# A graph attention kernel: one-hot picks from keys kept in DRAM, and one copy with three predicated copies in place of a mask and additions

## The chip, the cores and the metric

The kernel runs on one core of one Trainium2 chip. The metric is the device time of one execution in microseconds, the median of several runs.

## The reference

Three layers of a graph transformer over 6250 nodes of 64 features and 206250 edges, sorted by destination. Per layer:

```python
q, k, v = x @ Wq + bq, x @ Wk + bk, x @ Wv + bv
e = edge_attr @ We
alpha = sum(q[dst] * (k[src] + e), -1) / sqrt(64)
w = softmax of alpha over the edges of each dst
x = segment_sum((v[src] + e) * w, dst) + x @ Ws + bs
x = relu(x)            # and a layer norm with gamma and beta after layers 0 and 1
```

At the end `layernorm(x0 + log_softmax(x))`.

## The kernel before

Edges are cut into 403 chunks of 512, a chunk into four tiles of 128 edges (`T = 4`), and four chunks make a batch (`LB = 4`): 100 whole batches and a rest. Nodes stand in 49 blocks of 128. `x` of a layer lies in DRAM, and, split into two parts whose sum is exact enough, in SBUF as `parts` (18 low blocks and 18 high blocks).

The features of the source nodes, `x[src]`, reach the tile `feat` of a batch in one of two ways. A *gather* is an indirect DMA that POOL issues, one for each tile of 128 edges (L578). A *pick* computes the same rows on PE: a one-hot of the source node against `parts`. In layer 0 the edges of each chunk are sorted (`sorter`, class `Move`, with `hit` one-hots and matmuls at L993 and L1002) so that tile 0 of a chunk has only sources in the low blocks and tile 3 only sources in the high ones; only those tiles can be picked. `PICKS` says how many of the sixteen tiles of a batch are picked: 3 in layer 0 and 6 in layers 1 and 2; so 13 and 10 tiles are gathered.

A pick works in groups of two tiles of the same kind (class `Picker`). `aim` multiplies `coef` with the batch's codes (`to`, loaded whole from `toS`, 128 rows) to put each edge's key, the place of its source node, on all 128 partitions in PSUM (L1182, two matmuls), and DVE compares it with `rank` for five groups of four blocks at once, which makes `hot` (L1196). `batch` multiplies `hot` with `parts`, ten matmuls a tile, eight of 256 columns and two of 128 (L1218). The result `ps_x` (layer 0: `ps_s`) has rows of four candidate blocks for each edge; DVE multiplies them with a mask `which` (L1229) and adds them up in two steps (L1232, L1233), the last of which writes `feat`. `aim` for the next group is called as a group's matmuls begin, so its one-hot is emitted one group ahead.

The order of instructions on each engine is written out by hand. A unit (one batch) goes: `sums` of the unit two before (L1522), `weights` of the unit before (L1510, L1512), `scores` (L1484, L1488, then L1498 on DVE and the exponential L1502 on ACT), then four `turn`s, which transpose the gathered features of one chunk each (L1473 on PE, L1476 on ACT). Between the turns stand the picks of the next batch. After each turn ACT copies the index of a later chunk into a `gate` (L609), and the gathers of that chunk wait for it; in layers 1 and 2 it is the chunk two batches later. As a batch's node groups end, `finish` computes the new `x` (L1334 and following). In layer 0 the sorter's steps (`move`) stand between the turns as well, one whole move a unit.

DMAs other than the gathers go out on SP's and ACT's queues in program order. `drain` writes the sorted codes of a batch to `toS` (L1017, ACT's queue), and `decode` loads them (L1608, SP's queue) up to three units ahead into one of four `to` tiles, which both `aim` and `scores` read.

## Time and profile before

| | |
|---|---|
| time, median of 3 runs | 4654.81 us (4653.18 to 4660.39) |
| profiled execution | 4656.6 us, span 4654.9 us |
| PE busy | 4216.7 us (91%) |
| DVE busy | 3829.2 us (82%) |
| POOL busy | 3337.9 us (72%) |
| ACT busy | 1995.7 us (43%) |
| mean granted TensorE clock | 0.966 |
| layer 0, 1 and 2 | about 0 to 1900, 1950 to 3250, 3300 to 4600 us |

Layer boundaries show in the forty slices of the page as the two dips:

```profile
PE   6889999999999999689999999999699999999996
POOL 6777777777777766277777777777477777777774
```

Each digit is the busy share of a slice of 116 us in tenths. A row of a group reads: line, engine, operation, output and input tiles, shape, count, then busy time in total, mean ns of one, and after the second bar the idle time of the engine just before them and what ended it. PE's ends are modelled and overlap, so the text works with the time from one start to the next. POOL's instruction is the issue of the gather, not its transfer.

### The profile page before, as it was taken

Reading aid. Unit: us, or ns where it says so; the run is one execution under the profiler, and the core shown is the slowest. Engines: PE = TensorE matmul, PEld = TensorE weight load, DVE = VectorE, ACT = ScalarE, POOL = GpSimd, SP = SyncE. Lnnn points to the kernel's source line nnn. Section 1 sums busy time; section 2 is a strip of 40 time slices with the busy share of each in tenths; the row PEclk is TensorE's granted clock in tenths of the full one; section 3 lists DMA queues with packets and bytes.
Section 4 is the critical chain, followed back from the end, with each engine's and each line's share of the span. In section 5 each row is a group of like instructions: output and inputs, shape, how many; then the busy total and the mean of one; then the engine's idle time right before and its main releaser. Section 6 shows DMA issues by size and latency. Waiting matters only on the chain.

```text
span 4654.9 us, 117245 instructions
## 1 busy us (share of the span) xinstructions
PE 4216.7 (91%) x41145; PEld 3111.6 (67%) x41145; DVE 3829.2 (82%) x9064; ACT 1995.7 (43%) x5733; POOL 3337.9 (72%) x3390
## 2 busy tenths in 40 slices
PE   6889999999999999689999999999699999999996
PEld 3445555555555555367888888887478778878874
DVE  6778888898888888478888888888478888888885
ACT  2455555555555555333333333333234333334443
POOL 6777777777777766277777777777477777777774
PEclk9999999999999999799999999999799999999997
DMA  8787777777777777445555565555356655656553
GB/s 188 192 210 184 188 204 188 189 195 200 199 198 193 192 197 189 125 102 132 137 139 137 138 144 138 140 138 129 86 128 143 141 135 135 138 130 143 136 135 81
DMA packets 769749, 725.47 MB, mean 156 GB/s; under 512 B 403478, under 2 KB 544880, under 8 KB 769156
## 3 DMA queue, kind: packets, MB, share of 16 engines
q1 hardware_dynamic: 572564, 480.73, 43.5%
q0 software_dynamic: 108160, 110.97, 12.7%
q10 hardware_dynamic: 88432, 126.17, 7.7%
q8 instruction: 334, 5.47, 0.5%
q14 instruction: 259, 2.12, 0.2%
HBM read 557.62 MB, written 159.87 MB: 154 GB/s over the span
## 4 chain that ended last, share of the span: by engine, by line


## 5 line engine op out<-in xcount | busy, mean ns | idle before, releaser
L578 POOL DMA_INDIRECT feat<-x,gate x2004 | 1924.4, 960 | 613.9 <-issue 471.5
L578 POOL DMA_INDIRECT feat<-in_x,gate x1328 | 1365.8, 1028 | 526.2 <-issue 317.1
L1218 PE MATMUL ps_x<-parts,hot 128*128 128x256 f32 (+1 forms) x11880 | 1567.1, 288 | 0.0
L1218 PEld LDWEIGHTS ps_x<-parts,hot 128*128 128x128 f32 x11880 | 1457.1, 193 | 0.0
L1476 ACT COPY featT<-ps_a 64x256 f32<-64x256 f32 x2380 | 872.4, 367 | 1305.8 <-PE ps_a L1473 1265.2
L1196 DVE TENSOR_TENSOR hot<-ps_m,rank 128x1280 fp32r<-128x1280 f32 x594 | 879.9, 1481 | 33.1 <-PE ps_m L1182 32.9
L993 PE MATMUL ps_x<-hit,thirds 128*64 128x512 bf16 x4800 | 637.7, 393 | 5.5 <-DVE hit L983 5.1
L1473 PE MATMUL ps_a<-ident,feat 128*128 128x128 f32 x2380 | 488.0, 283 | 64.0 <-DMA feat<-x,gate 40.4
L983 DVE TENSOR_SCALAR hit<-ruler,pos 128x512 bf16<-128x512 f16 x1600 | 504.6, 363 | 1.7 <-PE ps_m L1002 1.5
L1473 PEld LDWEIGHTS ps_a<-ident,feat 128*128 128x128 f32 x2380 | 281.9, 140 | 333.4 <-issue 287.5
L1229 DVE TENSOR_TENSOR rows_of_b<-ps_x,which 128x512 f32<-128x512 f32 x594 | 406.4, 684 | 88.1 <-PE ps_x L1218 87.1
L1502 ACT ACTIVATE prob<-ps_s,part 128x512 f32<-128x512 f32 (+1 forms) x306 | 210.6, 688 | 625.6 <-DVE part L1500 500.0
L1218 PE MATMUL ps_s<-parts,hot 128*128 128x256 f32 (+1 forms) x2680 | 392.3, 294 | 30.9 <-ACT prob L1502 30.9
L993 PEld LDWEIGHTS <-thirds 128*64 128x64 bf16 x4800 | 233.2, 111 | 230.5 <-issue 83.6
L1218 PEld LDWEIGHTS ps_s<-parts,hot 128*128 128x128 f32 x2680 | 340.8, 195 | 60.7 <-ACT prob L1502 40.7
L1498 DVE TENSOR_REDUCE most<-ps_s 128x1 f32<-128x512 f32 (+1 forms) x306 | 211.2, 690 | 189.4 <-PE ps_s L1488 181.4
L1232 DVE TENSOR_TENSOR rows_of_b<-rows_of_b 128x256 f32<-128x256 f32 (+1 forms) x776 | 321.0, 414 | 26.6
L1522 PE MATMUL ps_g<-feat,probT 128*32 128x128 f32 x9672 | 338.2, 279 | 4.1 <-DVE y L1366 2.3
L1488 PE MATMUL ps_s<-featT,q 128*32 128x512 f32 x2418 | 336.3, 611 | 5.9 <-ACT featT L1469 5.2
L1522 PEld LDWEIGHTS ps_g<-feat,probT 128*32 128x32 f32 x9672 | 263.5, 111 | 52.6 <-issue 34.0
L1512 DVE COPY probT<-ps_p 128x512 f32<-128x512 f32 (+1 forms) x306 | 209.2, 684 | 99.0 <-PE ps_p L1510 97.3
L1182 PEld LDWEIGHTS <-coef 128*128 128x128 bf16 x1456 | 134.7, 99 | 190.5 <-issue 175.1
(226 smaller groups left out, 4392.6 us busy)
## 6 DMA issues: line engine op xcount, KB each, us to landing
feat<-eaP SPq DMA_DIRECT2D x296, 512.0 KB
featT<-eaS SPq DMA_DIRECT2D x296, 512.0 KB
raw<-in_ea SPq DMA_DIRECT2D x200, 256.0 KB
eaS<-eT ACTq DMA_DIRECT2D x200, 256.0 KB
eaP<-eN ACTq DMA_DIRECT2D x200, 256.0 KB
to<-toS SPq DMA_DIRECT2D x296, 128.0 KB
feat<-x,gate POOLq DMA_INDIRECT x2004
feat<-in_x,gate POOLq DMA_INDIRECT x1328
```

The lines of the kernel that those rows point to most:

```text
L578: nc.gpsimd.indirect_dma_start(out=feat[:, c, t, 0], out_offset=None, in_=xts[layer][:, :], in_offset=bass.IndirectOffsetOnAxis(ap=index[: ...
L983: nc.vector.tensor_scalar(hit, ruler, self.pos[:, at : at + 1], None, ALU.is_equal)
L993: nc.tensor.matmul(self.px[i][j * D : (j + 1) * D, :], self.thirds[i][:, part, (j * T + t) * D : (j * T + t + 1) * D], self.hits[t, 2 * i ...
L1196: nc.vector.tensor_tensor(hot, pk.unsqueeze(1).to_broadcast([P, NH, n * P]), rank.unsqueeze(2).to_broadcast([P, NH, n * P]), ALU.is_equal,)
L1218: nc.tensor.matmul(px[:, s, :w].rearrange("p b d -> p (b d)"), hot[:, h, s * P : (s + 1) * P], parts[:, i, b0 + h * KB : b0 + h * KB + w, ...
L1229: nc.vector.tensor_tensor(rows, px[:, :n], which[:, at : at + n, :].unsqueeze(3).to_broadcast([P, n, KB, D]), ALU.mult)
L1232: nc.vector.tensor_tensor(rows[:, :, : KB // 2], rows[:, :, : KB // 2], rows[:, :, KB // 2 :], ALU.add)
L1473: nc.tensor.transpose(pt[:, t // 2 * P : (t // 2 + 1) * P], rows[:, t * D : (t + 2) * D], ident)
L1476: nc.scalar.copy(featT[:, :, h, :], pt[h * D : (h + 1) * D, : T // 2 * P].rearrange("d (i e) -> d i e", e=P))
L1488: nc.tensor.matmul(self.p_s[slot(j) * W : (slot(j) + 1) * W, :], self.q[:, j * STRIDE : j * STRIDE + W], self.featT[:, j, :], start=False, ...
L1498: nc.vector.tensor_reduce(top[:n], self.p_s[:n], AX.X, ALU.max)
L1522: nc.tensor.matmul(p_g[rows, :].rearrange("n (h d) -> n h d", h=2), self.probT[:, t, rows], batch[:, c + j, t], start=(t == 0), stop=(t == ...
```

## The change

Keys: `Move.index` multiplies the sorted codes of tiles 0 and 3 with `keyc` (one matmul, 4 rows of 256), ACT copies the result as fp16 and writes it to `keyS` in DRAM; `decode` loads the keys of the picked tiles of a batch, broadcast to all 128 partitions, into one of two `keys` tiles. The key matmuls of each group (L1182) and `coef` are gone. The one-hot is made by five tensor_scalars, one for each group of four blocks, from `keys` in SBUF, for up to four tiles at a time; two rooms take turns, one of four tiles and one of three. Selection: ACT copies the first candidate block to `feat`, and DVE copies each of the other three over it where `which` says so. Still two tiles share one `ps_x`. `PICKS` becomes 3 in layer 0 and 7, 6, 7 in turn in layers 1 and 2, so that on average 9.33 tiles of a batch are gathered.

The codes for `scores` are now 24 rows for every unit (`toS` holds 4 x 6 rows of a batch, written by four DMAs instead of one, and loaded by a DMA in the unit before), and their matmul uses `codeT` in place of `codeS`. `decode` moves from the first turn of a unit, for the next three units, to the end of the unit, for units u+2 and u+3. To make room, `to` tiles go from 4 to 2, gates from 24 to 16, and set-up code (`locate`, `widen`) uses other tiles: `locate` one `w` tile in place of three `hot` tiles.

```diff
-PICKS = ((3,), (6,), (6,))
+PICKS = ((3,), (7, 6, 7), (7, 6, 7))
...
-            room = picks.tile([P, NH, 2 * P], F32R, name="hot").rearrange("p h e -> p (h e)").bitcast(F32)
+            room = nodes.tile([P, 2, GS, P], F32, name="w", bufs=1).rearrange("p h j c -> p (h j c)")
...
-            nc.scalar.dma_start(toS[self.k], self.to)
+            for c in range(LB):
+                nc.scalar.dma_start(toS[self.k, c], self.to[c * W : c * W + BITS + 1])
...
+            pk = pa[:LB, 2 * P :].rearrange("c (t e) -> c t e", t=2)
+            nc.tensor.matmul(
+                pk, keyc, self.to.rearrange("r (t e) -> r t e", t=T)[:, :: T - 1], start=True, stop=True
+            )
+            key = small.tile([LB, 2, P], FP16, name="key", bufs=1)
+            nc.scalar.copy(key, pk)
+            nc.scalar.dma_start(keyS[k].rearrange("t c e -> c t e"), key)
...
-            for s, c in enumerate(cs):
-                nc.tensor.matmul(
-                    pk[:, s * P : (s + 1) * P], coef[:, c, :], to[:, t * P : (t + 1) * P], start=True, stop=True
-                )
...
-            hot = picks.tile([P, NH, 2 * P], F32R, name="hot")[:, :, : n * P]
-            nc.vector.tensor_tensor(
-                hot,
-                pk.unsqueeze(1).to_broadcast([P, NH, n * P]),
-                rank.unsqueeze(2).to_broadcast([P, NH, n * P]),
-                ALU.is_equal,
-            )
+            room = (LB, MOST - LB)[self.turn]
+            hot = picks.tile([P, NH, room * P], F32R, name=f"hot{self.turn}", bufs=1)[:, :, : n * P]
+            self.turn = 1 - self.turn
+            for h in range(NH):
+                nc.vector.tensor_scalar(
+                    hot[:, h], keys[self.layer, k][:, first : first + n * P], rank[:, h : h + 1], None, ALU.is_equal
+                )
...
-                nc.vector.tensor_tensor(
-                    rows, px[:, :n], which[:, at : at + n, :].unsqueeze(3).to_broadcast([P, n, KB, D]), ALU.mult
-                )
-                nc.vector.tensor_tensor(rows[:, :, : KB // 2], rows[:, :, : KB // 2], rows[:, :, KB // 2 :], ALU.add)
-                nc.vector.tensor_tensor(
-                    loaded[self.layer, k][:, cs[0] : cs[0] + n, t, 0], rows[:, :, 0], rows[:, :, 1], ALU.add
-                )
+                        nc.scalar.copy(found, px[:, :n, 0])
+                        for b in range(1, KB):
+                            nc.vector.copy_predicated(
+                                found,
+                                which[:, at : at + n, b].bitcast(I32).unsqueeze(2).to_broadcast([P, n, D]),
+                                px[:, :n, b],
+                            )
...
-            if self.placed:
-                nc.tensor.matmul(self.p_s, codeS, self.to, start=True, stop=False)
-            else:
-                nc.tensor.matmul(self.p_s[:n], codeT[:k, :n], self.to[:k, :], start=True, stop=False)
+            nc.tensor.matmul(self.p_s[:n], codeT[:k, :n], self.to[:k, :], start=True, stop=False)
...
-            codes[layer, k] = tos.tile([P, CH], BF16, name="to")
-            nc.sync.dma_start(codes[layer, k], toS[k])
+            keys[layer, k] = picks.tile([P, MOST * P], FP16, name="keys", bufs=2)
+            nc.sync.dma_start(
+                keys[layer, k][:, : n * P],
+                keyS[k].rearrange("t c e -> (t c e)")[: n * P].partition_broadcast(P),
+            )
...
-            for k in range(u + 1, u + 4):
-                decode(layer, k)
...
+            for k in range(u + 2, u + 4):
+                decode(layer, k)
```

In the diff of the changed kernel line numbers shift by about 13; lines are cited by those of the kernel before.

More of the change, by code (lines that the diff above doesn't have):

```diff
@@ L41 @@
 BACK = 8
-PICKS = ((3,), (6,), (6,))
+PICKS = ((3,), (7, 6, 7), (7, 6, 7))
 LEAD = (4, 1, 1)
+MOST = max(n for p in PICKS for n in p)
 def slot(j):
@@ L509, in main_path @@
     feats = ctx.enter_context(tc.tile_pool(name="feats", bufs=FB))
-    tos = ctx.enter_context(tc.tile_pool(name="tos", bufs=4))
+    tos = ctx.enter_context(tc.tile_pool(name="tos", bufs=2))
     turns = ctx.enter_context(tc.tile_pool(name="turns", bufs=1))
@@ L515, in main_path @@
     sorts = ctx.enter_context(tc.tile_pool(name="sorts", bufs=2))
-    gates = ctx.enter_context(tc.tile_pool(name="gates", bufs=6 * LB))
+    gates = ctx.enter_context(tc.tile_pool(name="gates", bufs=4 * LB))
     nodes = ctx.enter_context(tc.tile_pool(name="nodes", bufs=2))
@@ L540, in main_path @@
     eaP = dram.tile([NT, P, LB * T * D], F32, name="eaP")
-    toS = dram.tile([NT, P, CH], BF16, name="toS")
+    toS = dram.tile([NT, LB, BITS + 1, CH], BF16, name="toS")
+    keyS = dram.tile([NT, 2, LB, P], FP16, name="keyS")
     xts = [x] + [dram.tile([NB * P, D], F32, name=f"x{i}") for i in range(1, L)]
@@ L725, in main_path @@
     )
-    fours = picks.tile([P, 2, KB, D], F32, name="rows_of_b", bufs=1).rearrange("p s b d -> p (s b d)")
+    fours = sorts.tile([P, 2 * T * D], F32, name="eN", bufs=1)
     fours = fours[:, :P].rearrange("p (a j) -> p a j", j=LB)
@@ L750, in widen @@
             nc.tensor.transpose(pw[:D, h * D : (h + 1) * D], ke[:, h, i, :], ident[:D, :D])
-        room = picks.tile([P, 2, KB, D], F32, name="rows_of_b", bufs=1).rearrange("p s b d -> p (s b d)")
+        room = sorts.tile([P, 2 * T * D], F32, name="eN", bufs=1)
         e, wqT = room[:D, :P], room[:D, P : P + D]
@@ L821, in main_path @@
     ones = const.tile([P, P], BF16, name="ones")
-    codeS = const.tile([P, P], BF16, name="codeS")
-    coef = const.tile([P, LB, P], BF16, name="coef")
+    keyc = const.tile([P, LB], BF16, name="keyc")
     pickc = const.tile([P, 2, LB], BF16, name="pickc")
-    kbs = const.tile([P, NT, 2, LB], BF16, name="kbs")
+    kbs = const.tile([P, NT, 2, LB], mybir.dt.uint8, name="kbs")
     four = const.tile([P, KB], F32, name="four")
@@ L833, in tools @@
         nc.vector.tensor_copy(four, ruler[:, :KB])
-        room = picks.tile([P, 2, KB, D], F32, name="rows_of_b", bufs=1).rearrange("p s b d -> p (s b d)")
-        two, wide = room[:, :LB], room[:, P : 2 * P]
         at = [ident[:, i::W] for i in range(ROW_K + 1)]
-        nc.vector.scalar_tensor_tensor(two, at[ROW_H], float(P), at[ROW_P], ALU.mult, ALU.add)
-        nc.vector.tensor_copy(coef, two.unsqueeze(2).to_broadcast([P, LB, P]))
+        nc.vector.scalar_tensor_tensor(keyc, at[ROW_H], float(P), at[ROW_P], ALU.mult, ALU.add)
         nc.vector.scalar_tensor_tensor(pickc[:, 0], at[ROW_B], float(P), at[ROW_P], ALU.mult, ALU.add)
         nc.vector.tensor_copy(pickc[:, 1], at[ROW_K])
-        nc.vector.memset(wide, 0.0)
-        for j in range(LB):
-            rows = slice(slot(j) * W, (slot(j) + 1) * W)
-            nc.vector.tensor_copy(wide[rows, j * W : j * W + BITS + 1], bit[rows, :])
-        pc = ps("a")
-        nc.tensor.transpose(pc[:, :P], wide, ident)
-        nc.vector.tensor_scalar(codeS, pc[:, :P], FAR, None, ALU.mult)
         for stamp in stamps:
@@ L1035, in index @@
             k = self.k
-            pi = ps("a")[:, : T * 2 * LB].rearrange("p (t v c) -> p t v c", t=T, v=2)
+            pa = ps("a")
+            pi = pa[:, : T * 2 * LB].rearrange("p (t v c) -> p t v c", t=T, v=2)
+            pk = pa[:LB, 2 * P :].rearrange("c (t e) -> c t e", t=2)
[5 more added lines that the diff above has]
+            nc.scalar.dma_start(keyS[k].rearrange("t c e -> c t e"), key)
             for t in range(T):
@@ L1162, in __init__ @@
                     cs = [c for c, i in those if i == t]
-                    self.todo += [(k, t, cs[i : i + 2]) for i in range(0, len(cs), 2)]
+                    self.todo += [(k, t, cs)] if cs else []
             self.aimed = []
             self.which = {}
-            self.side = 0
-            self.keys = ps("m") if layer else None
+            self.turn = 0
         def aim(self):
-            if not self.todo or (self.layer, self.todo[0][0]) not in codes:
+            if not self.todo or (self.layer, self.todo[0][0]) not in keys:
                 return
@@ L1174, in aim @@
             n = len(cs)
-            to = codes[self.layer, k]
-            if self.layer:
-                self.side = 1 - self.side
-                pk = self.keys[:, self.side * 2 * P :][:, : n * P]
-            else:
-                pk = ps("p")[:, : n * P]
-            for s, c in enumerate(cs):
-                nc.tensor.matmul(
-                    pk[:, s * P : (s + 1) * P], coef[:, c, :], to[:, t * P : (t + 1) * P], start=True, stop=True
-                )
+            first = LB * P if t else 0
             if (self.layer, k) not in self.which:
@@ L1210, in batch @@
                 self.aim()
-                n = len(cs)
-                px = ps("x" if self.layer else "s").rearrange("p (s b d) -> p s b d", s=2, b=KB)
                 b0 = RB if t else 0
-                for s in range(n):
+                for s, c in enumerate(cs):
+                    if s % 2 == 0:
+                        n = min(2, len(cs) - s)
+                        px = ps("x" if self.layer else "s").rearrange("p (s b d) -> p s b d", s=2, b=KB)
                     for m, h in enumerate((0, *reversed(range(1, NH)))):
@@ L1218, in batch @@
                             nc.tensor.matmul(
-                                px[:, s, :w].rearrange("p b d -> p (b d)"),
+                                px[:, s % 2, :w].rearrange("p b d -> p (b d)"),
                                 hot[:, h, s * P : (s + 1) * P],
@@ L1224, in batch @@
                             )
-                    if s + 1 < n:
-                        yield
-                at = (LB if t else 0) + cs[0]
-                rows = picks.tile([P, 2, KB, D], F32, name="rows_of_b", bufs=1)[:, :n]
-                nc.vector.tensor_tensor(
-                    rows, px[:, :n], which[:, at : at + n, :].unsqueeze(3).to_broadcast([P, n, KB, D]), ALU.mult
-                )
-                nc.vector.tensor_tensor(rows[:, :, : KB // 2], rows[:, :, : KB // 2], rows[:, :, KB // 2 :], ALU.add)
-                nc.vector.tensor_tensor(
-                    loaded[self.layer, k][:, cs[0] : cs[0] + n, t, 0], rows[:, :, 0], rows[:, :, 1], ALU.add
-                )
-                yield
+                    if s % 2 == n - 1:
+                        at = (LB if t else 0) + c - n + 1
+                        found = loaded[self.layer, k][:, c - n + 1 : c + 1, t, 0]
+                        nc.scalar.copy(found, px[:, :n, 0])
[5 more added lines that the diff above has]
+                            )
+                    yield
     def late():
@@ L1422, in __init__ @@
             self.plain = not layer and not self.placed
-            if self.placed:
-                self.to = codes[layer, self.k]
-                return
             self.to = tos.tile([P, CH], BF16, name="to")
-            nc.sync.dma_start(
-                self.to[: m * (BITS + 1), :], places[c : c + m].rearrange("c b e -> (c b) e")
-            )
+            here = toS[self.k] if self.placed else places[c : c + m]
+            nc.sync.dma_start(self.to[: m * (BITS + 1), :], here.rearrange("c b e -> (c b) e"))
         def ask(self):
@@ L1482, in scores @@
             self.p_s = ps("s")
-            if self.placed:
-                nc.tensor.matmul(self.p_s, codeS, self.to, start=True, stop=False)
-            else:
-                nc.tensor.matmul(self.p_s[:n], codeT[:k, :n], self.to[:k, :], start=True, stop=False)
+            nc.tensor.matmul(self.p_s[:n], codeT[:k, :n], self.to[:k, :], start=True, stop=False)
             for j in range(self.m):
@@ L1600, in move @@
             serve()
-    codes = {}
+    keys = {}
     def decode(layer, k):
-        if k < NT and placed(layer, k) and (layer, k) not in codes and (layer or k in moved):
-            codes[layer, k] = tos.tile([P, CH], BF16, name="to")
-            nc.sync.dma_start(codes[layer, k], toS[k])
+        n = picked(layer, k) if k < NT else 0
+        if n and (layer, k) not in keys and (layer or k in moved):
+            keys[layer, k] = picks.tile([P, MOST * P], FP16, name="keys", bufs=2)
[3 more added lines that the diff above has]
+            )
     class Line:
```

## The prediction

> **What bounds the kernel now.** First I read the groups of the page, to see which engine the picks and gathers occupy:

> ```profile
> L578 POOL DMA_INDIRECT feat<-x,gate x2004 | 1924.4, 960 | 613.9 <-issue 471.5
> L578 POOL DMA_INDIRECT feat<-in_x,gate x1328 | 1365.8, 1028 | 526.2 <-issue 317.1
> L1196 DVE TENSOR_TENSOR hot<-ps_m,rank 128x1280 fp32r<-128x1280 f32 x594 | 879.9, 1481 | 33.1 <-PE ps_m L1182 32.9
> L983 DVE TENSOR_SCALAR hit<-ruler,pos 128x512 bf16<-128x512 f16 x1600 | 504.6, 363 | 1.7 <-PE ps_m L1002 1.5
> ```

> A gather of layers 1 and 2 is 960 ns busy plus 306 ns idle (613.9/2004), with almost no other wait. Next the stretches, one inside each of layers 0, 1 and 2:

> ```profile
> 300.00:1800.00 1500.00, 1401.75 (x13821) 855.28 (x13815) 1297.63 (x3910) 798.25 (x2040) 1093.12 (x1076) 0.98 0.77 194
> 2100.00:3200.00 1100.00, 1046.91 (x10580) 883.55 (x10577) 950.70 (x1728) 411.52 (x1360) 834.87 (x870) 1.00 0.59 137
> ```

> Columns: PE, PEld, DVE, ACT, POOL busy, clock, DMA share, GB/s. In layer 1, 870 gathers in 1100 us are one in 1.264 us: POOL is full, and a batch (10 gathers) takes 12.64 us. But PE is busy 95% and DVE 86%, so the margin to the next engine decides. PE's timeline gives it, one batch from its sums to the next batch's:

> ```profile
> 2600.43 1.08 PE L1522 MATMUL ps_g<-feat,probT 128*32 128x128 f32 x32
> 2601.44 0.66 PE L1510 MATMUL ps_p<-ident,prob 128*128 128x128 f32 x4
> 2601.93 0.38 PE L1484 MATMUL ps_s<-to,codeS 128*128 128x512 bf16 x1
> 2602.24 1.07 PE L1488 MATMUL ps_s<-featT,q 128*32 128x512 f32 x8
> 2603.24 0.44 PE L1473 MATMUL ps_a<-ident,feat 128*128 128x128 f32 x2
> 2603.51 0.28 PE L1182 MATMUL ps_m<-to,coef 128*128 128x128 bf16 x2
> 2603.60 2.61 PE L1218 MATMUL ps_x<-parts,hot 128*128 128x256 f32 x20
> 2606.04 0.38 PE L1473 MATMUL ps_a<-ident,feat 128*128 128x128 f32 x2
> 2607.68 0.27 PE L1182 MATMUL ps_m<-to,coef 128*128 128x128 bf16 x2 [1.25 <-DVE hot L1196]
> 2607.76 2.60 PE L1218 MATMUL ps_x<-parts,hot 128*128 128x256 f32 x20
> ...
> 2613.30 0.32 PE L1522 MATMUL ps_g<-feat,probT 128*32 128x128 f32 x4
> ```

> From start to start: two picked tiles 2.44 us (2603.60 to 2606.04), so 1.22 each; two key matmuls 0.08 to 0.09. The batch spans 12.87 us, of which 1.38 is the wait at 2607.68, for a one-hot that DVE had late: 11.49 us of work. Eleven node groups a layer add some 2.4 us each (their matmuls by the same start times), 0.27 a batch: 11.76. PE has 0.9 us of slack a batch. The waits of the whole run agree: PE hardly waits for gathers, and waits longest for one-hots.

> ```profile
> PE ps_m L1182 <- DVE hot L1196: 101.7, 95, 2.0
> PE ps_a L1473 <- DMA feat<-x,gate: 40.4, 41, 3.3
> ```

> Layer 0 differs. There a batch takes 13 gathers x 1.394 us (1500/1076) = 18.1 us, of which 13 x 1.25 = 16.3 is the undisturbed pace. In the stretch above POOL waits 86.8 us for gates on ACT, PE waits 1.8 us for gathers: the compute chain, not POOL, sets layer 0, with about 0.9 us a batch before POOL would.

> **Layers 1 and 2, part by part, for a batch.**

> POOL: 6.67 picks leave 9.33 gathers. At 0.947 (the median; the mean has lock waits, below) + 0.305, that is 11.69 us, 0.95 less than now. This is the gain only if nothing else stands behind it.

> PE: 0.67 more picks x 1.22 = +0.81; six key matmuls go, 3 x 0.08 = -0.24. The scores' first matmul keeps its 128x512 moving operand, so no change. 11.76 + 0.57 = 12.33 us. PE passes POOL: of the 0.95 only 0.31 is left.

> DVE: out go three one-hots (start to start 1.40 each, 4.2) and three times multiply and two adds (0.71 + 0.46 + 0.21, 4.15). In come ten tensor_scalars with 128 elements a tile, from fp16 in SBUF, and 11 predicated copies. For the first no row has the same types. The nearest with one SBUF source and a pointer scalar are hit (345 ns median, 258 start to start, 512 elements, 16 bits in and out) and L1395 (247 ns, 160, 64 elements, fp32). L1369, a tensor_scalar on 256 fp32 in SBUF, took 293 ns at best where two-input L1359 took 425, so fp32 in SBUF goes at about two elements a cycle (1.9 a ns); L1395 then has a fixed 214 ns. A one-hot of four tiles is 480 ns (395 start to start), of three 412 (326), of two 345 (259): 5 x (0.395 + 2/3 x 0.326 + 1/3 x 0.259) = 3.5 us. Its lower bound, hit's own pace, is 2.3, its upper one, one element a cycle as L1196 runs, 5.7; fp32 out puts it by L1395. A predicated copy of 128 elements I take as L1233 (293 ns at 128), 0.31 with the 34 ns that dependent rows show, a single tile 0.24: 3.3 us a batch; if it took twice that, 6.6. DVE goes from 10.9 us (950.7/1100 of 12.64) to 9.4, or 11.6 at the first bound, 12.7 at the second, 14.9 at both, the last two above PE; I take the near rows. The next one-hot is started a whole item (3 or 4 tiles, 3.7 to 4.9 us of PE) ahead, its run lasting 2.1 us. So the 0.5 us a batch that PE waits for DVE should go, except where node groups crowd DVE.

> ACT: 3.67 copies of 0.27 (L1530), +1.0 on 4.7 us: hidden; it delays only the predicated copies behind it, and ps_x has two buffers, 2.4 us of PE.

> SP: the codes' DMA becomes two (keys, 128 x 1.75 KB; to, 24 KB), one issue of about 0.6 us more (L1608, 0.59), in an order that waits for stores anyway. Keys of u+3 are asked at the end of unit u and first read by DVE in the middle of unit u+1, some 6 us later; 229 KB at the stretch's 137 GB/s are 1.7 us, so I cost it at nothing. If it lands late, DVE waits in front of its predicated copies; two us a batch would still fit DVE's slack.

> What goes the other way is the lock between DVE and POOL. In the timeline:

> ```profile
> 2604.28 1.22 DVE L1334 TENSOR_TENSOR w<-both,mm 128x1024 f32<-128x1024 f32 x1
> 2604.45 1.87 POOL L578 DMA_INDIRECT feat<-x,gate  x1 [0.31 <-issue]
> ```

> That gather started under a DVE operation with two SBUF inputs and ended 0.92 us late. The excess is the time to the end of the DVE operation less 0.13 us; where DVE reads PSUM (L1196, 632 cases) it is 0. Gathers that started under a hit were 175 ns late on average (245 cases). So today's one-hots, which read PSUM, cost POOL nothing; the new ones read and write SBUF at two elements a cycle, five in a row. In 32 of 45 cases by the start times a gather got in between two hits in a row. With that rate a gather that meets a run of five loses about 0.2 us (four tiles), 0.15, 0.1; some 1.5, 1.3, 1 meet each: 0.46 us a batch. L1232 and L1233 stop locking (-0.1, already in the median). POOL: 11.69 + 0.46 + 0.06 (L1334) = 12.2 us, just under PE.

> [...]

> PE at 12.33 with 0.17 of leftover waits (node groups, POOL close behind) gives 12.5 against 12.64: -0.14 x 198 batches = -28 us. Bounds: -0.31 x 198 = -61, and the lock's, below.

> **Layer 0.** Picks stay at three. PE loses its waits around the key matmuls: 20.7 us for ps_p behind the one-hot, 34.6 from key matmul to first pick, 5.8 for probT, in 83 batches 0.7 us; DVE loses 4.4 and gains 3.0 us. Added on ACT a move: four DMA issues of 0.33 us (row ACTq L1017), a key copy of 0.4, two picked copies; ACT is 53% busy. Its cover is the idle behind the drain; if that is gone, 1.7 us x 100 = 170 us. The run of five locks POOL for 0.2 us more a batch, which gate waits absorb. I take half the waits, 0.4 x 96 = -38 us; bounds 0 and -0.75 x 96 = -72. At the start, locate has one room instead of three and waits for its own store: +3 us.

> **Sum.** 4656.6 (the profiled execution, span 4654.9; the median of the runs, 4654.8, is 1.8 less) - 28 - 38 + 3 = 4594, as a median 4592.

> **Rivals.**
> - Lock (slower), 0.22. No gather gets into a run of five. [...] A gather asks on average 0.63 us into the run: it loses 2.06 - 0.63 - 0.13 = 1.3 us for four tiles, 0.96 and 0.62 for three and two, 2.15 a batch. POOL then needs 13.9 us: +1.26 x 198 = +250, and layer 0's gain goes: 4905. It decides from 0.89 us a batch (12.64 - 11.75); at halfway, 1.5 us, +0.6 x 198 = +120 with no gain in layer 0: 4775. For: ends of copies that were passed over (L971 to L972, 38 of 38). Against: hit to hit.
> - Waits return, 0.16: predicated copies behind ACT and behind the five-run free ps_x late, PE at 12.7 to 12.8, layers 1 and 2 +20, layer 0 half: 4655. For: three dependent steps where one released ps_x. Against: two buffers and DVE's 1.5 us.
> - Both at the floor, 0.1: 4657 - 61 - 72 = 4524.
> - The copies or one-hots at their slow bounds, DVE above PE, 0.04: 12.7 to 14.9 us, +15 to +450.

> The forecast has 0.48, its own range 4545 to 4640. The whole range, 4525 to 4765, leaves out the upper half of the lock, most of the last rival and the floor's tail. Faster: 0.48 + 0.1 + a third of the second rival, 0.63; slower: lock, last rival and a little under half the second, 0.29; within 0.2% (9 us, about what a measurement here can tell from no change) 0.08.

> **What would show it.** Right: in layers 1 and 2 PE near 98% busy, POOL waiting for gates on ACT, gathers under 1.0 us, one-hots near 0.48 and 0.41 us, no PE wait for hot. Lock: gathers of 1.05 us and more, no gate waits, PE waiting for gathers. Waits: PE idle before ps_x matmuls, ended by DVE feat. A layer 0 not shorter than now, or ACT's issues in front of the gates, proves that part wrong.

## The result, and the profile after

| | before | changed kernel |
|---|---|---|
| time, median | 4657.60 us (4653.18 to 4667.33) | 4995.09 us (4988.68 to 5003.36, 4 runs) |
| ratio to before, 95% interval | | 1.0723, [1.0698, 1.0747] |
| profiled execution | 4656.6 us, span 4654.9 | 4994.19 us, span 4992.5 |
| mean granted TensorE clock | 0.966 | 0.924 |
| unit of layer 0 / 1 / 2, us | 18.39 / 12.68 / 12.67 | 22.10 / 12.41 / 12.38 |
| last row maximum of layer 0, us | 1960.0 | 2348.9 |

The forecast was 4592 us, faster. A unit here is the mean time from one batch's row maximum (`most`, L1498 before, L1481 after) to the next one's, without the first and last few of a layer. Lines of the changed kernel are its own: L580 is the gather (before L578), L1209 the pick matmul (L1218), L1189 the one-hot (L1196), L1035 the key copy, L1038 the index matmuls, L1513 the copy of the sums (L1530).

In the first four sets of experiments every kernel, the one before included, took 35 to 38% longer (the kernel before 6282 to 6421 us; a burst of 32 narrow matmuls at L1522 took 4.9 us in place of 1.08), for a cause that the traces do not settle, so a kernel there is compared only with others of its own set, and the last set, where the kernel before takes 4658 us again, gives the sizes.

The forty slices of the page of the changed kernel, each digit a share in tenths:

```profile
PE   5778888888888888886899999999969999999996
PEclk9888988889989888886999999999979999999998
```

Layers 1 and 2 (after the dip in the 19th slice, of 125 us each) have PE at 9 and a full clock. Layer 0 has grown from 17 slices of 116 us to 19 of 125; in it PE stands at 8, and the clock in most slices too, where before both stood at 9. The stretches say the same in numbers (PE, PEld, DVE, ACT, POOL busy, clock, DMA share, GB/s; layer 0, then layer 1):

```profile
300.00:1900.00 1600.00, 1375.27 (x12079) 840.85 (x12078) 1060.72 (x3685) 765.01 (x2029) 971.12 (x951) 0.88 0.62 156
2400.00:3500.00 1100.00, 1090.27 (x10838) 933.68 (x10840) 816.81 (x2531) 492.68 (x1715) 838.26 (x840) 1.00 0.64 147
```

In layer 1 PE is busy 99% and sets the pace; POOL is close behind it (9.33 gathers of 0.996 + 0.305 us are 12.1 of the 12.41 us). In layer 0 no engine is full. A layer-0 unit has the same PE instructions as before (167 against 169, counts by rate by unit), but PE is busy 19.0 us of its 22.10 (1375.27/1600) against 17.2 of 18.39, and idle 3.1 us against 1.2. So 1.9 us of the 3.7 are waits, and 1.8 are the same work taking longer, at a granted clock of 0.88 in place of 0.98.

The groups that answer those shown of before:

```profile
L580 POOL DMA_INDIRECT feat<-x,gate x1872 | 1864.2, 996 | 611.0 <-issue 409.6
L580 POOL DMA_INDIRECT feat<-in_x,gate x1328 | 1363.1, 1026 | 913.8 <-ACT gate L611 567.6
L1189 DVE TENSOR_SCALAR hot<-keys,rank 128x384 fp32r<-128x384 f16 (+3 forms) x2460 | 915.2, 437 | 0.0
```

A gather of layers 1 and 2 takes 996 ns in place of 960; one of layer 0 takes what it did (1026 against 1028), so the lock is not what lengthens layer 0. There POOL waits for gates on ACT (567.6 us), which says only that ACT is late. PE's own waits point at the cause (a row gives the total in us, the number of waits and the longest):

```profile
PE ps_a L1038 <- ACT key L1035: 235.0, 95, 6.1
PE ps_a L1331 <- DVE w L1327: 37.9, 6, 9.6
```

In 95 of the 100 moves PE stops in front of the index matmuls until ACT has copied the keys. `index` puts keys and indices into one PSUM tile: the key matmul writes its upper half, ACT reads that half, and the index matmuls write the lower half behind it. One such stop, by the changed kernel's timeline (DMA issues are on ACTq):

```profile
1000.43 1.44 ACTq L1009 DMA_DIRECT2D toS<-to  x2
...
1001.96 1.02 ACTq L1012 DMA_DIRECT2D eaS<-eT  x2
...
1003.02 0.27 ACT L1513 COPY part<-ps_g 128x128 f32<-128x128 f32 x1 [2.33 <-DMA toS<-to]
...
1004.71 1.28 ACT L1288 ACT_TABLE_LOAD   x1
...
1005.14 0.27 PE L1031 MATMUL ps_a<-to,keyc 128*4 128x256 bf16 x1
...
1006.83 0.60 ACT L954 CAST thirds<-raw 128x512 bf16<-128x512 f32 x1
...
1007.45 0.36 ACT L1035 CAST key<-ps_a 4x256 f16<-4x256 f32 x1
...
1007.87 0.25 PE L1038 MATMUL ps_a<-pickc,to 128*128 128x8 bf16 x4 [2.45 <-ACT key L1035]
```

The key matmul starts at 1005.14 and takes 0.27 us. ACT reaches the copy at 1007.45, since in its own order a table load, an activation and a cast stand ahead of it; PE, whose next matmul waits for that copy, does nothing for 2.45 us. The table load comes in few of the moves, but the pattern is general: over all 100 moves 204 us pass between the end of the key matmul and the start of the copy, and for 153 of them ACT is busy with work that stands ahead in its order, above all the casts of `thirds` (52 us), the copies of `featT` (39) and the exponentials with their sums (40). DMA issues add some 11 us.

The first rows show a second thing: after the drain's copies ACT issues four stores of codes where there was one (the row shows the last two), and ACT has stood idle for 2.33 us when its next work starts; in a drain of the kernel before at about the same time it was 0.40 us:

```profile
1005.64 0.33 ACTq L1017 DMA_DIRECT2D toS<-to  x1
...
1006.99 0.27 ACT L1530 COPY part<-ps_g 128x128 f32<-128x128 f32 x1 [0.40 <-ACT eT L1016]
```

And this is how the clock goes around PE's stop (stretches of 4 us of the changed kernel around it, same columns):

```profile
1004.00:1008.00 4.00, 1.55 (x15) 0.87 (x14) 3.45 (x19) 3.13 (x7) 2.44 (x3) 0.89 0.91 230
1008.00:1012.00 4.00, 4.00 (x33) 2.33 (x31) 1.01 (x7) 0.88 (x2) 0.40 (x1) 0.50 0.24 51
1012.00:1016.00 4.00, 4.00 (x28) 2.83 (x28) 3.90 (x16) 1.73 (x5) 0.95 (x1) 0.76 0.00 0
1016.00:1020.00 4.00, 4.00 (x37) 2.74 (x34) 3.69 (x14) 2.51 (x7) 2.85 (x3) 1.00 0.39 94
```

PE works 1.55 us of the first stretch, and then, although it is busy throughout, gets half the clock. In this trace every record of the clock is either full or half (111 of each), so twice the lost share of the first three stretches is the time at half clock: 0.9 + 4.0 + 1.9 = 6.8 us. The clock's records say the same of the other stops: 86 of the 100 waits in front of the index matmuls began at full clock, and in 80 of these cases the clock fell to half during the wait or within 3.4 us of its end (the shortest record of the clock is 3.41 us). These stretches, 523 us in all, are about a third as long as layer 0's time at full clock (1683 us) and hold 80 of its 100 falls. So here a stop of PE is paid about twice, once as idle time and once as slower work, which is what the 1.9 and 1.8 us of a unit say for layer 0 as a whole.

### The profile page after: what moved, and what is told of

Same layout as the page of the kernel before. It is cut to its first block, busy times and chain, and to the rows that moved or that the text cites. A ratio compares the mean times of both kernels' runs of the same rounds, so it can differ in the third digit from the quotient of the medians.

```text
span 4992.5 us, 121087 instructions
## 1 busy us (share of the span) xinstructions
PE 4452.2 (89%) x41108; PEld 3294.3 (66%) x41108; DVE 3389.4 (68%) x11137; ACT 2239.7 (45%) x6741; POOL 3275.7 (66%) x3258
## 4 chain that ended last, share of the span: by engine, by line
## 5 line engine op out<-in xcount | busy, mean ns | idle before, releaser
L580 POOL DMA_INDIRECT feat<-x,gate x1872 | 1864.2, 996 | 611.0 <-issue 409.6
L580 POOL DMA_INDIRECT feat<-in_x,gate x1328 | 1363.1, 1026 | 913.8 <-ACT gate L611 567.6
L1209 PE MATMUL ps_x<-parts,hot 128*128 128x256 f32 (+1 forms) x13200 | 1712.2, 286 | 31.9 <-DVE feat L1221 15.4
L1209 PEld LDWEIGHTS ps_x<-parts,hot 128*128 128x128 f32 x13200 | 1603.7, 191 | 53.1 <-ACT feat L1219 30.7
L1189 DVE TENSOR_SCALAR hot<-keys,rank 128x384 fp32r<-128x384 f16 (+3 forms) x2460 | 915.2, 437 | 0.0
L1221 DVE COPY_PREDICATED feat<-which,ps_x 128x128 f32<-128x128 int32 (+1 forms) x2178 | 616.4, 288 | 378.6 <-ACT feat L1219 317.7
L984 PE MATMUL ps_x<-hit,thirds 128*64 128x512 bf16 x4800 | 680.1, 414 | 3.1 <-DVE hit L974 3.1
L1209 PE MATMUL ps_s<-parts,hot 128*128 128x256 f32 (+1 forms) x2680 | 469.6, 332 | 1.7 <-ACT eN L1020 1.5
L1219 ACT COPY feat<-ps_x 128x128 f32<-128x128 f32 (+1 forms) x726 | 186.5, 257 | 627.8 <-PE ps_x L1209 620.1
L1209 PEld LDWEIGHTS ps_s<-parts,hot 128*128 128x128 f32 x2680 | 408.4, 230 | 69.9 <-issue 52.5
L1481 DVE TENSOR_REDUCE most<-ps_s 128x1 f32<-128x512 f32 (+1 forms) x306 | 211.2, 690 | 227.1 <-PE ps_s L1471 220.8
L1221 DVE COPY_PREDICATED feat<-which,ps_s 128x64 f32<-128x64 int32 (+1 forms) x546 | 143.3, 262 | 317.6 <-ACT feat L1219 301.4
```

Of the source, the lines that this page charges most:

```text
L580: nc.gpsimd.indirect_dma_start(out=feat[:, c, t, 0], out_offset=None, in_=xts[layer][:, :], in_offset=bass.IndirectOffsetOnAxis(ap=index[: ...
L984: nc.tensor.matmul(self.px[i][j * D : (j + 1) * D, :], self.thirds[i][:, part, (j * T + t) * D : (j * T + t + 1) * D], self.hits[t, 2 * i ...
L1189: nc.vector.tensor_scalar(hot[:, h], keys[self.layer, k][:, first : first + n * P], rank[:, h : h + 1], None, ALU.is_equal)
L1209: nc.tensor.matmul(px[:, s % 2, :w].rearrange("p b d -> p (b d)"), hot[:, h, s * P : (s + 1) * P], parts[:, i, b0 + h * KB : b0 + h * KB + ...
L1221: nc.vector.copy_predicated(found, which[:, at : at + n, b].bitcast(I32).unsqueeze(2).to_broadcast([P, n, D]), px[:, :n, b],)
L1481: nc.vector.tensor_reduce(top[:n], self.p_s[:n], AX.X, ALU.max)
```

## The experiments

The theory after this reading: layer 0 is lost to the index matmuls' wait for the key copy, and to the half clock behind it. Rivals: ACT is late by the four store issues, whatever PE waits for; or by the picked copies that stand ahead of the gates. The expectations of the first two sets are given for a kernel before of 4655 us, so in those sets only the order of the kernels, their units and their waits can be held against them.

**Set 1** (kernel before 6420.79 us). *Keys last* moves the key matmul, its copy and its store behind the four index matmuls:

```diff
-            nc.tensor.matmul(
-                pk, keyc, self.to.rearrange("r (t e) -> r t e", t=T)[:, :: T - 1], start=True, stop=True
-            )
-            key = small.tile([LB, 2, P], FP16, name="key", bufs=1)
-            nc.scalar.copy(key, pk)
-            nc.scalar.dma_start(keyS[k].rearrange("t c e -> c t e"), key)
             for t in range(T):
...
+            nc.tensor.matmul(
+                pk, keyc, self.to.rearrange("r (t e) -> r t e", t=T)[:, :: T - 1], start=True, stop=True
+            )
+            key = small.tile([LB, 2, P], FP16, name="key", bufs=1)
+            nc.scalar.copy(key, pk)
+            nc.scalar.dma_start(keyS[k].rearrange("t c e -> c t e"), key)
```

> Against the changed kernel the key matmul stands behind the four index matmuls (L1038), so that these no longer wait for ACT to copy the keys. Theory A (PE stands in the middle of the sorter until ACT, with its drain and other copies in front, has copied the keys out of the shared PSUM tile: 235 us, 95 waits, and the idle PE loses clock, 0.88 in layer 0): layer 0 falls from 22.1 us a unit to 18.5 to 19.5, the clock in 300:1900 rises over 0.94, time 4650 to 4740. Rival B (the four stores of codes and the key store on ACT's queue, 0.33 us each, hold ACT's chain; the wait only moves to the next user of ps_a or to the gates): at most 100 us less, 4895 to 4995. Rival C (one-hots in SBUF lock out the gathers): no change, 4995.

Measured: 6342.41 us, 0.9895 [0.9852, 0.9938]; layer-0 unit 24.00 us. PE's wait for the key copy is gone.

*One store* writes the codes by one DMA of 128 rows, as before, and `scores` loads its 24 rows out of it; the rest is the changed kernel:

```diff
-            for c in range(LB):
-                nc.scalar.dma_start(toS[self.k, c], self.to[c * W : c * W + BITS + 1])
+            nc.scalar.dma_start(toS[self.k], self.to)
```

> Against the changed kernel the sorted codes go out in one DMA of 128 rows as before the change, and the load takes the 24 rows out of them; the wait for the keys stays. Theory A: ACT reaches the key copy some 1 us earlier a unit, so the wait shrinks by up to 1 us of 2.4: 4890 to 4970, with L1038 still waiting over 120 us. Rival B: the loss goes, 4650 to 4750. Rival C: 4995.

Measured: 6462.83 us, 1.0063 [1.0037, 1.0090]; unit 25.33 us.

*First copy on DVE* takes the picked copy of layer 0 off ACT:

```diff
-                        nc.scalar.copy(found, px[:, :n, 0])
+                        if self.layer:
+                            nc.scalar.copy(found, px[:, :n, 0])
+                        else:
+                            nc.vector.tensor_copy(found, px[:, :n, 0])
```

> Against the changed kernel the first candidate block in layer 0 is copied by DVE instead of ACT (two copies a batch), so that ACT no longer stands at a picked tile (189.7 us of waiting for ps_s in 300:1900) in front of the gates. Theory A: that wait is only ACT's idle time; 4960 to 5000. Rival D (gates and key copies are late since ACT stands at picked tiles): 4700 to 4900. Rival C: 4995.

Measured: 6453.33 us, 1.0048 [1.0029, 1.0066]; unit 25.38 us. And all three edits together:

> All three edits at once. Theory A: all of the gain of the first edit and little more: within 40 us of e1_keys_last, 4610 to 4700. If each edit takes away a part of one chain on ACT, the sum of the three gains of the single runs is more than this one's gain; if they are separate, equal to it.

Measured: 6401.34 us, 0.9971 [0.9947, 0.9995]; unit 24.97 us.

What follows: with the keys last a layer-0 unit is 1.3 us shorter than with either of the other two, in which PE's wait for the key copy stays (223.7 and 254.8 us). The other two, put on top of keys last, take back 59 us, where within 40 us was expected. The changed kernel was not run in this set; if it stands 107 us above keys last, as it does in set 3, it would be at 6449 us (an estimate), and one store and the first copy on DVE gain nothing.

**Set 2** repeats two of them on another chip (kernel before 6422.04 us):

> The kernel of e1_keys_last once more, in another set of runs, since in that set the kernel before took 6421 us and PE ran much of the time at half clock, which hides a wait of 2 us a unit. Theory A (PE's wait for the key copy and the clock it costs are most of the loss in layer 0): ratio to the kernel before 1.00 to 1.02 against 1.072 for the changed kernel, 4650 to 4750. Rival B (the wait only moves, ACT's stores are the cause): 1.05 to 1.07.

Measured: 6337.70 us, 0.9891 [0.9841, 0.9940].

> The kernel of e4_all_three once more (keys last, one store of codes, first copy of layer 0 on DVE). Theory A: within 40 us of the first of this call. Rival B: over 100 us below it.

Measured: 6395.14 us, 0.9965 [0.9941, 0.9989]: 57 us above keys last, which is neither of the two expectations. The order of set 1 is confirmed; that the two added edits cost time is not explained.

**Set 3** (kernel before 6282.29 us) has the changed kernel as control.

> The changed kernel as it is, as the control for the other three on the same chip. If the lost time lies in layer 0 alone, as the first two traces have it (a unit there 22.1 us against 18.4, layers 1 and 2 at 12.4 against 12.7), this is slower than the kernel before by 7 per cent where the kernel before takes 4655 us, and by the same 300 to 400 us where it takes longer. If instead the loss came and went with the run, it is within 1 per cent of the kernel before.

Measured: 6407.07 us, 1.0206 [1.0168, 1.0243]: 125 us slower than before, not 300 to 400.

> The key matmul, its copy on ACT and its store behind the four index matmuls. Theory (the index matmuls wait on PE for ACT's copy of the keys, 6.1 us in a unit, and the clock falls after it): faster than the changed kernel by 100 us at least, a layer-0 unit shorter by over 1 us, and the wait of the index matmuls on the key copy is gone. Rival (ACT is late by its four store issues, whatever PE waits for): no faster than the changed kernel by more than 30 us, since the wait only moves to the next matmuls that need ACT.

Measured: 6300.57 us, 1.0022 [0.9996, 1.0048]: 107 us less than the control, as the theory has it. But the layer-0 unit is only 0.7 us shorter (24.44 against 25.11), less than expected. (The 6.1 us of the expectation is the longest single wait; the mean is 235.0/95 = 2.5 us.)

*Key copy on DVE*, everything else in its place:

```diff
-            nc.scalar.copy(key, pk)
+            nc.vector.tensor_copy(key, pk)
```

> The key matmul stays ahead of the four index matmuls, in their PSUM tile; only its copy moves from ACT to DVE. Theory: what PE waits for is ACT's place in its own order (the copy stands behind the drain's casts, six DMA issues and the thirds); DVE reaches the copy earlier, so the wait shrinks to 1 or 2 us and the layer-0 unit is shorter by 0.5 to 1.2 us (50 to 120 us in all), with the store on ACT waiting for DVE as the price. Rival (the wait is the tile's, whichever engine copies): as the changed kernel within 30 us.

Measured: 6361.59 us, 1.0129 [1.0091, 1.0167]: 45 us less than the control, a little under the theory's range. PE's wait for the copy fell from 237.4 us in 82 waits to 178.4 in 77, or from 2.9 to 2.3 us each, just above the 1 to 2 us expected: DVE is late as well.

> The kernel before, unchanged, for its profile on this chip: ratio 1.000. Where it takes 4655 us, units of 18.4, 12.7 and 12.7 us in the three layers; where it takes 6420 us, the units tell in which layers the other 1760 us lie, and so what the experiments before this one were compared with.

Measured: 6284.57 us, 1.0005 [0.9986, 1.0024], with units of 23.45, 17.96 and 18.08 us: about 5 us more in a unit of every layer, with the kernel before itself, and so no part of the change.

**Set 4** (kernel before 6289.26 us) asks whether the wait or the order does it. *Keys in a tile of their own* leaves the key matmul first:

```diff
-            pk = pa[:LB, 2 * P :].rearrange("c (t e) -> c t e", t=2)
+            pk = ps("a")[:LB, 2 * P :].rearrange("c (t e) -> c t e", t=2)
```

> The key matmul stays first, but writes a PSUM tile of its own (the other buffer of the same pair), so that the four index matmuls need not wait for ACT's copy of the keys. Theory (the loss is that wait, not the place in the order): as with the keys last, within 40 us of it in this set, and no wait of the index matmuls on the key copy. Rival (ACT's lateness comes out wherever PE next needs ACT): within 30 us of the changed kernel, 1.015 to 1.025 of the kernel before if it stands as in the set before this one, since the next transposes then wait for the second buffer instead.

Measured: 6334.42 us, 1.0069 [1.0045, 1.0094]. PE's wait for the key copy is gone; a wait of the index matmuls for `featT` (114.5 us), which now frees their buffer, has come in.

> The kernel with the keys last, again, as what the other three of this set are compared with: 0.985 to 1.005 of the kernel before, as in the sets before.

Measured: 6316.23 us, 1.0049 [1.0015, 1.0082]; 18 us less than the own tile, with intervals that overlap. The changed kernel was not run in this set; it stood at 1.0206 in set 3, and the rival had the own tile at 1.015 to 1.025. As far as ratios of two sets can be compared, the wait on the shared tile is what costs, not the place in the order, and that rival is out.

*Keys last, and the first copy of layer 0 on DVE* (the third edit of set 1):

> Keys last, and in layer 0 the first block's copy on DVE in place of ACT. Theory of a residue on ACT (with the wait gone, layer 0 is still 1 us a unit over the kernel before since the picked copies stand ahead of the gates on ACT): 40 to 100 us faster than keys last alone. Rival (the gates wait for PE, not for the copies): within 20 us of it, or up to 30 us slower for the added DVE work.

Measured: 6320.67 us, 1.0058 [1.0033, 1.0083]: nothing gained. Taking the picked copies off ACT, at the price of the same work on DVE, does not remove the residue.

*Keys last, and layer 0's picks in the PSUM buffer of the transposed probabilities*:

```diff
-                        px = ps("x" if self.layer else "s").rearrange("p (s b d) -> p s b d", s=2, b=KB)
+                        px = ps("x" if self.layer else "p").rearrange("p (s b d) -> p s b d", s=2, b=KB)
```

> Keys last, and in layer 0 the pick matmuls write the PSUM buffer of the transposed probabilities in place of that of the scores. Theory of a residue in PSUM (the pick matmuls wait 30 us for the predicated copies and the scores wait for the same buffer): 20 to 80 us faster than keys last alone. Rival (the other buffer is as busy, or the wait has cover): within 20 us, or slower by up to 60 us.

Measured: 6293.64 us, 1.0026 [1.0003, 1.0050]: 23 us less than keys last, but the intervals overlap; undecided.

**Set 5** (kernel before 4658.21 us) gives the sizes.

> The changed kernel as it is, beside keys last in the same set: 1.015 to 1.025 of the kernel before where that takes 6280 us and more, 1.07 where it takes 4655 us.

Measured: 4987.98 us, 1.0706 [1.0688, 1.0724].

> Keys last, in the same set as the changed kernel. Theory: 80 to 130 us less than it where the kernel before takes 6280 us and more; if the kernel before takes 4655 us, some 300 us less than it, with a layer-0 unit back at 18 to 19 us.

Measured: 4723.10 us, 1.0134 [1.0117, 1.0151]: 265 of the 330 us come back, somewhat less than the 300 expected, and the layer-0 unit is 19.31 us against the control's 22.03 (18 to 19 expected). Layer 0 of control and keys last, in that order, by the stretch from 80 to 1900 us:

```profile
80.00:1900.00 1820.00, 1547.25 (x13454) 931.00 (x13457) 1195.66 (x4150) 853.07 (x2247) 1104.07 (x1074) 0.88 0.62 157
80.00:1900.00 1820.00, 1648.96 (x15320) 972.76 (x15318) 1363.91 (x4725) 962.38 (x2562) 1249.81 (x1219) 0.95 0.70 178
```

In the same time PE does 14% more matmuls (15320 against 13454) with 7% more busy time; the rest is the clock. The granted clock of the trace is either full or half, so 0.88 is 24% of the stretch at half speed and 0.95 is 10%. PE's largest waits in the page of keys last:

```profile
PE ps_a L1331 <- DVE w L1327: 38.1, 6, 9.9
PE ps_s L1209 <- ACT prob L1485: 32.3, 32, 2.4
PE ps_a L1032 <- ACT featT L1462: 29.7, 20, 2.8
```

The control's 240.5 us of waiting for the key copy are gone, and no single wait of that size has come in their place (L1032 are its index matmuls). Not all of it is gained: from 80 us to the last row maximum of layer 0 PE is idle for 350 us in the control, 208 with the keys last and 158 in the kernel before, so about 100 of the 240 us come back as smaller waits. At half clock are 572, 237 and 122 us of the same time.

*Six picks in every batch of layers 1 and 2*, the changed kernel otherwise:

```diff
-PICKS = ((3,), (7, 6, 7), (7, 6, 7))
-MOST = max(n for p in PICKS for n in p)
+PICKS = ((3,), (6,), (6,))
+MOST = 7
```

> The changed kernel with six picks in every batch of layers 1 and 2 in place of 6.67, the rest as it is. If POOL sets those layers, two thirds of a gather more is 0.67 x (1.00 + 0.30) = 0.87 us a batch, 170 us in all, on top of the changed kernel; if PE sets them, a pick less is 0.67 x 1.3 = 0.87 us a batch off; if neither does (both idle by a fifth and more, as in the last sets), within 60 us.

Measured: 5090.67 us, 1.0923 [1.0905, 1.0941]: 103 us over the control, between the expectations for POOL (170) and for neither (under 60). Its units of layers 1 and 2 are 12.94 and 13.00 us, the control's 12.40 and 12.41. Its gathers, and the transposes, where PE waits for gathers for 213.8 us (40.4 in the kernel before):

```profile
L580 POOL DMA_INDIRECT feat<-x,gate x2004 | 1984.6, 990 | 611.1 <-issue 442.1
L1459 PE MATMUL ps_a<-ident,feat 128*128 128x128 f32 x2380 | 533.0, 294 | 240.8 <-DMA feat<-x,gate 213.8
```

PE now waits for gathers, so POOL is the bound. The count of gathers and the idle time before them are those of the kernel before (2004, 613.9 us); each takes 990 ns in place of 960. That is 30 ns x 9.8 gathers a batch (2004 in the 204 batches of both layers) = 0.30 us, and the unit is 0.30 us longer than before's (12.97 against 12.67). That the lock makes the difference can be read from the single gathers of layers 1 and 2: the 500 that started under a one-hot took 1081 ns on average, the 685 that started while DVE did nothing 946, and in the kernel before the 708 that started under a one-hot, which then read PSUM, took 946 as well. So at an equal share of picks the new selection costs 0.30 us a batch by the lock and saves no time, POOL being the bound; the larger share then takes 0.56 off, until PE is full.

*Keys last, picks on the other buffer, and two picks in layer 0*:

```diff
-PICKS = ((3,), (7, 6, 7), (7, 6, 7))
+PICKS = ((2,), (7, 6, 7), (7, 6, 7))
```

> Keys last, picks of layer 0 on the other PSUM buffer, and two picks a batch in layer 0 in place of three. A pick is ten matmuls on PE (1.3 us in layer 1 at full clock), a gather 1.03 + 0.3 us on POOL. If PE sets layer 0, 1.3 to 1.9 us a unit off, 110 to 170 us less than keys last and below the kernel before; if POOL's gathers set it, 1.3 us a unit more, 110 us slower than keys last.

Measured: 4687.97 us, 1.0059 [1.0039, 1.0079]: 35 us less than keys last, a third of the least that was expected of PE as the bound. Two things differ from keys last here, and the other buffer alone gave 23 us in set 4 (undecided), so the run does not tell what one pick less is worth; only that it did not cost the 110 us of gathers as the bound. The unit is 18.83 us, the nearest to before's 18.39 in this set. No kernel of this set beats the kernel before. In sets 1 and 2 keys last was 1.1% below it, in sets 3 and 4 0.2 to 0.5% above.

## Why the prediction was wrong, point by point

| part | forecast, us | measured, us |
|---|---|---|
| layers 1 and 2 | -28 (floor -61) | -49 (control: 2530.2 for both, first to last row maximum, against 2579.2) |
| layer 0 | -38 (bounds 0 and -72) | +379, with the start (control: its last row maximum at 2339.1 against 1960.0) |
| start | +3 | +3 (first row maximum at 74.9 against 72.0) |

**Layers 1 and 2** went by their steps. PE became the bound, with 99% busy where "near 98%" was forecast, 12.40 us a batch for 12.5; no wait for hot is left. The one-hots of four, three and two tiles take 478, 410 and 344 ns in the median (forecast 480, 412 and 345), a predicated copy of 128 elements 300 (310). The lock was put at 0.46 us a batch over gathers of 0.947 us: some 2.7 gathers a batch that meet a one-hot, 0.17 us each. In the control 2.5 gathers a batch started under a one-hot (505 in both layers) and took 0.15 us more than the 0.947, 0.38 us a batch; the mean gather came out at 0.996 us where 0.947 + (0.46 + 0.06)/9.33 = 1.00 was forecast. One sign came out weakly: POOL waited for gates on ACT for only 13.5 of the 1100 us from 2300 us on, since POOL is nearly full itself. Leftover waits of 0.17 were too many (12.33 + 0.17 against 12.40); that is most of the difference between -28 and -49.

**The rival lock fell.** It needed 2.15 us a batch and gathers of 1.05 us and more; they take 1.00. Under one long instruction the trace of the changed kernel shows a larger loss (the 22 gathers of layers 1 and 2 that started under L1324, 128x1024 on SBUF, took 1.25 us on average, against 0.945 of those that started while DVE did nothing); a gather which started in a run of five short ones lost 0.15 us on average, where being held to the end of the run would have cost it 0.6 to 1.3 by the prediction's working. So gathers do get in between the instructions of a run. **Waits return** did not happen in layers 1 and 2: PE waits 31.9 us in the whole run in front of the pick matmuls into `ps_x`.

**Layer 0 is the step that failed**, in the sentence "Added on ACT a move: four DMA issues of 0.33 us (row ACTq L1017), a key copy of 0.4, two picked copies; ACT is 53% busy." It counted the key copy by its duration, on ACT, where it has cover. It did not name the wait that the change adds on another engine: on PE the index matmuls stand behind a copy in ACT's order, since both write one PSUM tile. The changed kernel's own `index` shows this: `pi` and `pk` are two views of `pa`. The price that it gave if ACT's cover were gone, 170 us, was also too small: the stop costs 265 us with the half clock behind it (control less keys last), 2.65 us a move. And the half clock behind a wait of PE stands in no term of the sum. The runs tell it from its rivals: with the keys last or in a tile of their own the wait goes, with the copy on DVE it shrinks, and each time the kernel is faster (the own tile only by ratios of two sets, 1.007 against the changed kernel's 1.021); with one store in place of four, or the picked copy off ACT, the wait stays. That the clock's part is caused by the stop is read from the stretches, from the 80 of 86 stops with a fall of the clock at or right behind them, and from the clock's return once the stop is gone (0.88 to 0.95); it was not varied by itself.

**What stays open**: 65 us of the 330 remain with the keys last, all of it in layer 0 (in its profiled execution +121 there and -52 in layers 1 and 2). So the stop is the larger part of what failed and not all of it: without it layer 0 is still 121 us longer, where 38 less was forecast. PE is idle there for 49 us more than in the kernel before (208 against 158), and the 115 us more at half clock (237 against 122) are worth up to 58; these are the two parts, and their cause is not known. ACT's late start after the drain (2.33 us against 0.40 in the timelines above) is one suspect; with the keys last it still waits there, 32 times in the stretch from 300 to 1800 us:

```profile
ACT part L1513 <- DMA toS<-to: 96.8, 32, 5.6
```

Over the 100 drains ACT stands idle before its next work for 66 us in the kernel before, 256 in the control and 274 with the keys last, so this idle time came with the change and did not go with the stop. But in set 1 one store in place of four cut it (181 us, and 199 with all three edits, against 365 with the keys last alone), and the kernel was not faster for it. The runs speak against this suspect, though one store was not tried where the kernel before takes 4658 us. Keys last together with a tile of their own was not tried.

One slip in the prediction's chances changes nothing here: 0.22 + 0.04 and "a little under half" of 0.16 are 0.33 for slower, not 0.29.

## What to carry to other kernels

When a change adds work to an engine that has slack, look first at who waits for it: in a kernel whose order is written out by hand, a copy costs the place it has in its engine's order, on every engine that stands behind it; here a copy of 0.36 us held PE for 2.5 us a move. In this kernel two results in one PSUM tile were one dependency, though they lie in different halves: PE waited 235.0 us for the copy of the one before it wrote the other, and with a tile for each that wait was gone. Share of work (picks against gathers) and the way the work is done are two changes; run them apart, as six picks did here, or a gain from the one hides a loss from the other.
